# Splitting the first norm's statistics between two engines, and reordering two steps of the last image, in a four-layer convolution network

## The chip, the cores and the metric

The kernel runs on one core of a Trainium2 chip. The metric is the device time of one execution in microseconds (us); the time before is the median of three runs, 3094.22 us (3093.67 to 3095.54). All data is fp32. The core's engines each work through their own queue of instructions in order: TensorE (PE, with its weight loads shown as PEld), VectorE (DVE), ScalarE (ACT), GpSimd (POOL) and SyncE (SP, which here only issues DMA transfers).

## The reference, cut to what matters

Four images of 256 channels and 64x64 pixels pass through four residual layers. What the change touches are two group norms inside layer 0 (`gn1` and `gn2`, eight groups of 32 channels each), the `_gn` between layers 0 and 1 (32 groups of 8 channels), and the inverse norms of the pixels in layer 1 (`rmsnorm`).

```python
def group_norm(x, w, b):                      # layer 0, 8 groups
    mean = xg.mean(axis=(2, 3, 4)); var = xg.var(axis=(2, 3, 4))
    return (xg - mean) * rsqrt(var + 1e-5) * w + b

# layer 0
xs = relu(group_norm(conv3x3(x, smooth_w) + smooth_b, gn1_w, gn1_b))
f = theta(xs) @ phi(xs)                       # 4096 x 4096 per image
y = softmax(f, axis=-1) @ g(xs)
out0 = group_norm(conv1x1(y, w_w, w_b), gn2_w, gn2_b) * 0.1 + xs
# layer 1
xn = rmsnorm(x, g_norm)                       # x / |x| over the channels of a pixel
q, k, v = conv1x1(xn, w_qkv)
out1 = rmsnorm(w_out @ linear_attention(softmax_d(q), softmax_n(k), v) + b_out, g_out)
# layer 2: a depthwise and a 1x1 convolution with generated weights; layer 3: mixed experts
x = x + out0(_gn(x)); x = x + out1(_gn(x)); x = x + out2(_gn(x)); x = x + out3(_gn(x))
```

## The kernel before

**Tiles.** 256 channels are two halves of 128 partitions (`NH = 2`); an image is 4096 columns per half. A k4 tile holds 128x1024 fp32, from a ring of nine; PSUM banks hold 128x512, a ring of eight. The order of the instructions on every engine is the order in which the program writes them down (a manual schedule); nothing is reordered afterwards.

**Stages.** `convolve_first` makes the 3x3 convolution of image 0 alone, since nothing else is there to run; `project` makes theta, phi and g; then `attend(b)` runs the 4096x4096 attention of image b in 8 blocks of 512 columns. Beside `attend(b)` runs a chain with the later layers of image b-1 and the convolution of image b+1. Behind the last image's attention there is no other attention: `tail` of image 3 (`nonlocal_out`, `linear_attention`, `generated`, `mixed`) runs alone, with the 16 pieces of image 2's layer 3 (`held`, matmuls into `ps_ex`) handed in by `w.fill(n)` to give PE something to do, and added to the result on DVE by `w.settle()`.

**The end of `convolve_first`.** The image's rows lie as `image[:, oh, :, k, :]`, four sets k of 16 rows for each channel half oh. After the last products, DVE joins row set 4 into the image (`rows_joined(4, oh, ...)`, six operations of 128x1024 for each half), then runs 12 `bn_stats` (128x512 each, for k = 0, 1, 2), four additions of the last products from PSUM (`tt(y, y, ps, ...)`, for k = 3), and 4 more `bn_stats`. `normed_relu` then calls `group_finish`: `bn_aggr` per half (L339), the bias added to the mean (L124), a matmul with an averaging matrix for the mean over the group (`pm`, L344), the deviations (`ev`), a matmul for the variance (`pv`, L355), and a power of -0.5 on POOL (L217). The affine factors follow, then the ReLU on ACT (L676), and `project` (L879).

**The last image's second norm.** `group_finish(wy_stats[b], ...)` runs as above on the attention's output, with the last two products of the output with the residual (`multiply`, L905, DVE 128x512 each) put in between. The mean and variance of the sum (norm output + residual), which the next norm (`_gn` of layer 1) needs, are not measured but worked out from the two means, variances and their covariance: about 20 DVE operations of 128x2 each, between the first norm's factor `rstd` and the next norm's `pm`. In them both the mean and the variance are complete (L1050 to L1055, tile `mv_in`; the profile shows them under the helpers L124 and L127) before `pm` starts. Two `bn_aggr` of the residual (L1043, `rmv`) lie there too. The addition itself (`on_the_way`, 128x512 and 128x1024 pieces on DVE) is done step by step by `next(sums)`.

**The loop over q, k, v.** `linear_attention` takes the image in 8 chunks of 512 columns. For each: `normed(c)` (ACT: two 128x512 normalisations L1102, a square L1104; DVE: the sum `s2`), `norms` (PE: eight small matmul instructions into `ps_ss`, L1112; DVE: a maximum, L1114; POOL: power -0.5, L217), `qkv` (PE: four products into `ps_qkv`, L1126; ACT: Exp and copy with the inverse norms `rinv` as scale, L1130 and L1131; DVE: sums and scaling of q, L1136 and L1137), and `context` (PE L1145, L1148). From chunk 1 on `norms` is called one chunk ahead. For chunk 0 it is called inside `qkv`, so that its DVE maximum stands behind what the loop's first pass has put into DVE's queue:

```python
        for c in range(NC):
            if c + 1 < NC:
                ahead = normed(c + 1)
            if alone:
                next(sums, None)
            yield 0.5
            this = yield from qkv(*ready)
```

`alone` is true for the last image only.

Of the kernel before, what the change touches and what calls it, by code (L numbers as in the profile page):

```python
# [8 lines left out]
F32 = mybir.dt.float32  # L9
# [84 lines left out]
def conv_preact_fast(ctx: ExitStack, tc: tile.TileContext, guard, x, wc, wtpg, ww, wqkv, wout, w1cat, wd2,  # L94
# [25 lines left out]
    def bank(name):  # L120
        return pp.tile([P, 512], F32, tag="bank", name=name, bufs=8)

    def tt(o, a, b, op):
        nc.vector.tensor_tensor(o, a, b, op)  # L124

    def stt(o, a, s, b, op0, op1):
        nc.vector.scalar_tensor_tensor(o, a, s, b, op0, op1)  # L127
# [199 lines left out]
    def stats_tile():  # L327
        return sp.tile([P, NH, 8, 6], F32, name="st")

    def group_finish(st, avg, eps, shift=None, between=()):  # L330

        if callable(st):
            mv = st()
        else:
            mv = sp.tile([P, NH, 2], F32, name="mv")
            for h in range(NH):
                nc.vector.bn_aggr(mv[:, h, :], st[:, h, :, :].rearrange("p c s -> p (c s)"))  # L339
        if shift is not None:  # L340
            tt(mv[:, :, 0], mv[:, :, 0], shift, ALU.add)
        yield 1
        pm = bank("pm")
        nc.tensor.matmul(pm[:, 0:NH], avg, mv[:, :, 0], start=True, stop=True)  # L344
        gm = sp.tile([P, NH], F32, name="gm")
        nc.vector.tensor_copy(gm, pm[:, 0:NH])
        ev = sp.tile([P, NH], F32, name="ev")
        tt(ev, mv[:, :, 0], gm, ALU.subtract)
        tt(ev, ev, ev, ALU.mult)
        tt(ev, ev, mv[:, :, 1], ALU.add)  # L350
        for f in between[0:1]:
            f()
        yield 1
        pv = bank("pv")
        nc.tensor.matmul(pv[:, 0:NH], avg, ev, start=True, stop=True)  # L355
        rstd = sp.tile([P, NH], F32, name="rstd")
        nc.vector.tensor_scalar(rstd, pv[:, 0:NH], eps, None, ALU.add)  # L357
        rsqrt(rstd, rstd)
        for f in between[1:]:
            f()  # L360
        return mv, gm, rstd
# [451 lines left out]
    def convolve_first(w):  # L813

        def go(ops):
            for op, *args in ops:
                op(*args)

        def across_all(a, rows):
            return [(a, k, across_plain(k, rows), lambda oh, h, k=k: u[a](k, oh, h)) for k in ACROSS1]  # L820

        filter_down((0,))
        _, gm, rstd = yield from input_stats()
        yield from normalise(gm, rstd)
        st = stats_tile()
        products, joined, row_products, rows_joined, _, stats = joiner(st)
        keep((0,))
        go(down_plain(0, ra))
        filter_down((1, 2))
        go(down_plain(1, rb))  # L830
        filter_down((5,))
        filter_down((3, 4))
        u = {a: filter_across(a) for a in (2, 4, 3)}
        keep((1, 2, 5, 3, 4))
        copy_x(0)

        for t in (rb, rc):
            nc.gpsimd.memset(t[:, :, :, 0:1], 0.0)
            nc.gpsimd.memset(t[:, :, :, HW + 1:HW + 2], 0.0)
        row_products(0, ra)  # L840
        go(down_plain(2, ra, rb))
        row_products(1, rb)
        go(down_plain(3, rc))
        last = [(a, k, products(a, k, v, f)) for a, k, v, f in across_all(2, ra)]
        for row, rows in ((3, rc), (4, rb)):
            this = across_all(row, rows)
            if row == 3:
                go(down_plain(4, rb, rc))
            else:
                go(down_plain(5, ra))  # L850
            for i, (a, k, v, f) in enumerate(this):
                if i + 1 < TX1:
                    t = joined(*last[i + 1])
                this[i] = (a, k, products(a, k, v, f))
            if row == 3:
                for oh in range(NH):
                    rows_joined(2, oh, t[oh])
            last = this
        y3 = row_products(5, ra)
        for i in range(1, TX1):  # L860
            t = joined(*last[i])
        for oh in range(NH):
            rows_joined(4, oh, t[oh])
        for j in range(3):
            stats(j)
        for y, ps in y3:
            tt(y, y, ps, ALU.add)
        stats(3)
        yield from normed_relu(w, 0, st)


    def project():
# [21 lines left out]
    res_st = cp.tile([P, NH, NQ, 6], F32, name="res_st")  # L894
    joint = cp.tile([P, NH, NQ], F32, name="joint")
    pivot_in = cp.tile([P, NH], F32, name="pivot_in")
    last_block = []

    def attend(b):

# [73 lines left out]
        for i in range(NQ * NM):  # L974
            q, m = divmod(i, NM)
            if m == 0:
                py = bank("py")
                tot = k4("tot")
            if i + 1 < NQ * NM:
                logits(i + 1)  # L980
            for s in range(2):
                nc.tensor.matmul(py, g[:, bass.ts(2 * m + s, P)], probs[i][:, bass.ts(s, 512)],  # L982
                                 start=(m == 0 and s == 0), stop=(m == NM - 1 and s == 1))
            if m == 1:
                tt(tot, probs[i - 1], probs[i], ALU.add)
            elif m > 1:
                tt(tot, tot, probs[i], ALU.add)
            if b == B - 1 and m == 9:
                xc = k4("xc").rearrange("p (h n) -> p h n", h=NH)
                nc.sync.dma_start(out=xc, in_=xs_d[b].rearrange("h p n -> p h n")[:, :, bass.ts(q, 512)])  # L990
            if b == B - 1 and m in (12, 14):
                h = m // 2 - 6
                nc.vector.bn_stats(res_st[:, h, q, :], xc[:, h, :])
            for t in todo:
                next(t, None)
            if m == NM - 1:
                todo = [ended(q, py, tot, xc)]
                next(todo[0])
            yield i + 1 < NQ * NM
# [6 lines left out]
    def nonlocal_out(w, b, big, k4, xs_in):  # L1006
# [26 lines left out]

        if xs_in is not None:

            mv = sp.tile([P, NH, 2], F32, name="mv_in", bufs=1)
            rmv = sp.tile([P, NH, 2], F32, name="rmv", bufs=1)
            cov = sp.tile([P, NH], F32, name="cov", bufs=1)
            off = sp.tile([P, NH], F32, name="off_in", bufs=1)
            tt(mv[:, :, 0], wmv[:, :, 0], bias, ALU.subtract)  # L1040
            tt(off, mv[:, :, 0], pivot_in, ALU.add)
            for h in range(NH):
                nc.vector.bn_aggr(rmv[:, h, :], res_st[:, h, :, :].rearrange("p c s -> p (c s)"))  # L1043
            nc.vector.tensor_reduce(cov, joint, AX.X, ALU.add)
            tt(off, off, rmv[:, :, 0], ALU.mult)
            stt(cov, cov, 1.0 / N, off, ALU.mult, ALU.subtract)
        sc, sh = affine(gm, rstd, vec_s[:, V_G2W, :], vec_s[:, V_G2B, :], bias, 0.1)
        if xs_in is not None:
            w.fill(1)
            tt(mv[:, :, 0], mv[:, :, 0], sc, ALU.mult)  # L1050
            tt(mv[:, :, 0], mv[:, :, 0], rmv[:, :, 0], ALU.add)
            tt(mv[:, :, 1], wmv[:, :, 1], sc, ALU.mult)
            stt(mv[:, :, 1], cov, 2.0, mv[:, :, 1], ALU.mult, ALU.add)
            tt(mv[:, :, 1], mv[:, :, 1], sc, ALU.mult)
            tt(mv[:, :, 1], mv[:, :, 1], rmv[:, :, 1], ALU.add)  # L1055

            def on_the_way():

# [14 lines left out]
                        added(2 * c + h, sc)  # L1073
                    yield

            return (lambda: mv), sh, on_the_way()
        w.fill(2)
        for i, (c, h) in enumerate(PARTS):
            added(i, sc)
# [10 lines left out]
    def linear_attention(w, b, big, qT, k4, st, sh, sums):  # L1090

        alone = sums is not None
        _, gm, rstd = yield from group_finish(st, avg8, 1e-5, sh, (lambda: next(sums),) * 2 if alone else ())
        nb = norm_bias(gm, rstd, sh)
        pctx = bank("ps_ctx")
        NC = N // 512
# [18 lines left out]
            rsqrt(rinv, rinv)  # L1115
            return rinv

        def qkv(xg, s2, rinv):

            qk = k4("qk").rearrange("p (j o) -> p j o", j=4)  # L1120
            v1 = k4("v1")[:, 0:4 * (P + 1)].rearrange("p (j o) -> p j o", j=4)
            nc.gpsimd.memset(v1[:, :, P:P + 1], 1.0)
            for j in range(4):
                ps = bank("ps_qkv")
                for h in range(NH):
                    nc.tensor.matmul(ps[:, 0:3 * HID], xg[:, h, bass.ts(j, P)], wqkv_s[:, h, :],  # L1126
                                     start=(h == 0), stop=(h == NH - 1))
                if rinv is None:
                    rinv = norms(s2)
                nc.scalar.activation(qk[:, j, :], ps[:, 0:2 * HID], AF.Exp, scale=rinv[:, j:j + 1])  # L1130
                nc.scalar.activation(v1[:, j, 0:P], ps[:, 2 * HID:3 * HID], AF.Copy, scale=rinv[:, j:j + 1])  # L1131
                yield 0.125
# [19 lines left out]
            w.fill(1)  # L1152
        w.settle()
        ahead = normed(0)
        if alone:
            next(sums)
        yield 1
        ready = *ahead, None
        last = None
        for c in range(NC):  # L1160
            if c + 1 < NC:
# [448 lines left out]
    def tail(b, big, qT, k4=k4, diag=None, xs_in=None, held=None):  # L1610

        def layers(w):
            st, sh, sums = yield from nonlocal_out(w, b, big, k4, xs_in)
            st = yield from linear_attention(w, b, big, qT, k4, st, sh, sums)
            st, sh = yield from generated(w, b, big, k4, st, sh, diag)
            if b + 2 < B:
                load_x(b + 2)
            elif b + 2 == B:
# [642 lines left out]
```

## Time and profile before

| | us |
|---|---|
| median of three runs | 3094.22 (3093.67 to 3095.54) |
| the profiled execution, its time | 3093.8 |
| its span, first to last instruction | 3091.9 |
| PE busy | 3001.9 (97%) |
| DVE busy | 2130.8 (69%) |
| ACT busy | 1152.7 (37%) |
| POOL busy | 131.9 (4%) |

Times in the views below count from the span's start. In a row of the timeline the first number is the start, the second the length from the first start to the last end, then engine, line, operation, output<-inputs, shapes, count; the bracket gives how long the engine had been idle before it and whose end released it. The mean granted TensorE clock of the execution is 0.993. Outside the two stretches that the change touches (118 to 143 us, and 2816 to 2864 us) the profile shows DVE, ACT and PE working through the attention at a steady pace.

### The profile page before, as it was taken

The page shows a single profiled execution, that of the slowest core. Times are in us where ns is not written, and L with a number is a line of the kernel's source. Part 1 is how long each engine was busy: PE and PEld are TensorE (multiplying, and loading weights), DVE is VectorE, ACT ScalarE, POOL GpSimd, SP SyncE. Part 2 cuts the span into 40 slices and gives each one's busy share as a digit, 9 for nine tenths or more (in the row PEclk, how much of TensorE's full clock was granted, in tenths as well). Part 3 has the DMA queues.
Part 4 walks back from the last instruction along what each step waited for, and adds up shares of the span by engine and source line. Part 5 has one row for each costly group of instructions (what it writes and reads, how often), then busy time and mean ns, then how long its engine had stood idle before and what let it go on. Part 6 is the DMA issues. An engine that isn't in the chain of part 4 may idle for free.

```text
span 3091.9 us, 24448 instructions
## 1 busy us (share of the span) xinstructions
PE 3001.9 (97%) x8606; PEld 1484.7 (48%) x8606; DVE 2130.8 (69%) x2773; ACT 1152.7 (37%) x2139; POOL 131.9 (4%) x178
## 2 busy tenths in 40 slices
PE   6899999999999999999999999999999999998998
PEld 3354555445554444444565444444546544444643
DVE  8747777853547996777536797678463669875485
ACT  2134333353555332323364432222346443333621
POOL 0100000000010000000011000000001100000100
PEclk9999999999999999999999999999999999999999
DMA  5234011122100023113300101311420000022021
GB/s 219 78 100 142 31 45 38 34 51 72 58 11 28 14 75 125 35 41 65 116 1 11 35 19 70 126 41 38 95 82 14 18 28 28 14 89 82 8 68 66
DMA packets 61088, 178.44 MB, mean 58 GB/s; under 512 B 6560, under 2 KB 16544, under 8 KB 56736
## 3 DMA queue, kind: packets, MB, share of 16 engines
q1 hardware_dynamic: 56928, 160.04, 15.1%
q0 software_dynamic: 4032, 16.78, 2.9%
q8 instruction: 70, 1.15, 0.2%
q14 instruction: 58, 0.48, 0.1%
HBM read 115.45 MB, written 78.12 MB: 63 GB/s over the span
## 4 chain that ended last, share of the span: by engine, by line
PE 78%; DVE 15%; issue 5%; ACT 1%; POOL 0%; DMA 0%; POOLq 0%; ACTq 0%; DVEq 0%
PE pf L926 23%; PE py L982 22%; PE ps_qkv L1126 5%; PE ps_conv L504 4%; PE ps_tp L879 4%; DVE dw L127 4%; PE ps_ex L1574 3%; DVE tot L124 3%; PE ps_pw L1374 3%; PE ps_conv L576 2%; PE ps_g L884 2%; PE ps_wy L963 2%; PE ps_o L1201 1%; PE ps_dw L1419 1%; DVE big L127 1%
## 5 line engine op out<-in xcount | busy, mean ns | idle before, releaser
L927 ACT ACTIVATE pr<-pf 128x512 f32<-128x512 f32 x1024 | 604.0, 597 | 1195.4 <-PE pf L926 1148.8
L926 PE MATMUL pf<-tpg 128*128 128x512 f32 x2048 | 969.3, 596 | 2.9 <-ACT pr L927 2.9
L982 PE MATMUL py<-pr,tpg 128*128 128x512 f32 x2048 | 962.4, 592 | 2.5 <-ACT pr L927 2.3
L124 DVE TENSOR_TENSOR tot<-tot,pr 128x1024 f32<-128x1024 f32 x448 | 546.1, 1219 | 175.2 <-ACT pr L927 174.0
L982 PEld LDWEIGHTS py<-pr,tpg 128*128 128x128 f32 x2048 | 388.9, 190 | 494.7 <-issue 477.6
L926 PEld LDWEIGHTS pf<-tpg 128*128 128x128 f32 x2048 | 381.9, 190 | 438.2 <-issue 412.1
L127 DVE SCALAR_TENSOR_TENSOR dw<-xp,dk,dw 128x1008 f32<-128x1008 f32 x208 | 262.9, 1267 | 9.9 <-ACT dw L1366 7.0
L504 PE MATMUL ps_conv<-v,u 128*128 128x512 f32 x384 | 171.0, 593 | 3.6 <-DVE v L124 3.6
L1126 PE MATMUL ps_qkv<-wqkv_s,xg 128*128 128x384 f32 x384 | 129.9, 487 | 0.0
L124 DVE TENSOR_TENSOR tpg<-ps_g,bg_s 128x512 f32<-128x512 f32 x32 | 22.1, 691 | 145.6 <-PE ps_g L884 145.6
L879 PE MATMUL ps_tp<-big,wtpg_s 128*128 128x512 f32 x256 | 118.0, 605 | 3.0 <-ACT big L676 3.0
L504 PEld LDWEIGHTS ps_conv<-v,u 128*128 128x128 f32 x384 | 72.7, 190 | 96.4 <-issue 89.8
L217 POOL TENSOR_TENSOR rstd<-rstd,half 128x2 f32<-128x2 f32 x24 | 17.5, 730 | 2347.5 <-DVE rstd L357 2230.5
L955 DVE RECIPROCAL inv<-pss 128x512 f32<-128x512 f32 x31 | 103.9, 3351 | 5.5 <-PE pss L938 5.5
L1374 PE MATMUL ps_pw<-dw,pk 128*128 128x512 f32 x224 | 101.4, 592 | 0.0
L1126 PEld LDWEIGHTS ps_qkv<-wqkv_s,xg 128*128 128x128 f32 x384 | 72.2, 190 | 53.5 <-issue 9.8
L1136 DVE TENSOR_REDUCE qs<-qk 128x16 f32<-128x512 f32 x24 | 16.5, 686 | 117.4 <-ACT qk L1130 117.4
L880 ACT ACTIVATE tpg<-ps_tp,btp_s 128x512 f32<-128x512 f32 x64 | 43.8, 686 | 119.6 <-PE ps_tp L879 119.6
L879 PEld LDWEIGHTS ps_tp<-big,wtpg_s 128*128 128x128 f32 x256 | 47.9, 195 | 55.0 <-issue 50.6
L1203 ACT ACTIVATE junk<-ps_o 128x256 f32<-128x256 f32 x128 | 49.1, 384 | 64.0 <-PE ps_o L1201 59.4
L1130 ACT ACTIVATE qk<-ps_qkv,rinv 128x256 f32<-128x256 f32 x96 | 45.5, 474 | 72.6 <-PE ps_qkv L1126 60.2
L124 DVE TENSOR_TENSOR v<-ra 128x1024 f32<-128x1024 f32 x58 | 69.6, 1221 | 0.4
(343 smaller groups left out, 3125.3 us busy)
## 6 DMA issues: line engine op xcount, KB each, us to landing
xp<-in_x_dram SPq DMA_DIRECT2D x16, 1024.0 KB, 6.4
wy_d<-wt SPq DMA_DIRECT2D x32, 512.0 KB, 2.9
wy<-wy_d SPq DMA_DIRECT2D x32, 512.0 KB, 4.0
out_dram<-res SPq DMA_DIRECT2D x64, 256.0 KB, 2.0
xs_d<-big POOLq DMA_DIRECT2D x24, 512.0 KB, 11.4
u<-filters SPq DMA_DIRECT2D x48, 256.0 KB, 2.5
xs<-xs_d SPq DMA_DIRECT2D x24, 512.0 KB, 4.8
u<-rows_d SPq DMA_DIRECT2D x36, 256.0 KB, 3.0
```

The costliest lines, as they stand in the source:

```text
L124: nc.vector.tensor_tensor(o, a, b, op)
L127: nc.vector.scalar_tensor_tensor(o, a, s, b, op0, op1)
L504: nc.tensor.matmul(ps[oh], u(oh, h), v[:, bass.ts(h, 512)], start=(h == 0), stop=(h == NH - 1))
L576: nc.tensor.matmul(ps[:, bass.ts(oh, IY * IX)], u[i][:, h, bass.ts(oh, P)], v[:, i, bass.ts(h, IY * IX)], start=(h == 0), stop=(h == NH - 1))
L879: nc.tensor.matmul(ps, wtpg_s[:, h, k, :], big[:, h, cols], start=(h == 0), stop=(h == NH - 1))
L926: nc.tensor.matmul(pf, phi[:, bass.ts(2 * m + s, P)], theta[:, bass.ts(q, 512)], start=True, stop=True)
L927: nc.scalar.activation(pr[:, bass.ts(s, 512)], pf, AF.Exp)
L955: nc.vector.reciprocal(inv, pss)
L982: nc.tensor.matmul(py, g[:, bass.ts(2 * m + s, P)], probs[i][:, bass.ts(s, 512)], start=(m == 0 and s == 0), stop=(m == NM - 1 and s == 1))
L1126: nc.tensor.matmul(ps[:, 0:3 * HID], xg[:, h, bass.ts(j, P)], wqkv_s[:, h, :], start=(h == 0), stop=(h == NH - 1))
L1374: nc.tensor.matmul(ps, pk[:, h * NH * P + oh * P:h * NH * P + (oh + 1) * P], dw[h][:, bass.ts(s, 512)], start=(h == 0), stop=(h == NH - 1))
L1574: nc.tensor.matmul(ps, wm[h][:, bass.ts(oh, P)], big[:, h, bass.ts(c, 512)], start=(h == 0), stop=(h == NH - 1))
```

## The change

Three parts. First, `convolve_first`: DVE takes `bn_stats` of the row sets 0 and 3 only. For each half, right after its join, the two `bn_stats` of row set 0 are aggregated into a `pivot`, whose negated mean is the bias of two ACT passes (Identity and Square) over each of the row sets 1 and 2, summed by the accumulator into `sums`. `moments` combines the two sources; `group_finish` takes it in place of the statistics tile. Second, for the last image, the residual's `bn_aggr` and two constants (`residual_known`) are moved into the attention's last block; the mean of the sum is worked out first and given to `pm`, the variance is worked out by `late()` behind `pm`, and the shift `sh` in the `between` step of the second norm. Third, for the last image, the first chunk's first product and its `norms` are written ahead of the loop.

```diff
+    def aggregated(st):
+        mv = sp.tile([P, NH, 2], F32, name="mv")
+        for h in range(NH):
+            nc.vector.bn_aggr(mv[:, h, :], st[:, h, :, :].rearrange("p c s -> p (c s)"))
+        return mv
...
+        mv, late = st() if callable(st) else aggregated(st), None
+        if isinstance(mv, tuple):
+            mv, late = mv
...
         nc.tensor.matmul(pm[:, 0:NH], avg, mv[:, :, 0], start=True, stop=True)
+        if late is not None:
+            var = late()
+        else:
+            var = mv[:, :, 1]
...
-        tt(ev, ev, mv[:, :, 1], ALU.add)
+        tt(ev, ev, var, ALU.add)
...
+        def half(oh, k):
+            for s in range(2):
+                nc.vector.bn_stats(st[:, oh, k // 3 * 2 + s, :], image[:, oh, bass.ts(s, IY // 2), k, :])
+
         for oh in range(NH):
             rows_joined(4, oh, t[oh])
-        for j in range(3):
-            stats(j)
-        for y, ps in y3:
+            half(oh, 0)
+            nc.vector.bn_aggr(pivot[:, oh, :], st[:, oh, 0:2, :].rearrange("p c s -> p (c s)"))
+            nc.vector.tensor_scalar(minus[:, oh:oh + 1], pivot[:, oh, 0:1], -1.0, None, ALU.mult)
+            for k in (1, 2):
+                for i, f in enumerate((AF.Identity, AF.Square)):
+                    nc.scalar.activation(k4("about").rearrange("p (y x) -> p y x", x=HW), image[:, oh, :, k, :], f,
+                                         bias=minus[:, oh:oh + 1], accum_out=sums[:, i, oh, k - 1:k])
+        for i, (y, ps) in enumerate(y3):
             tt(y, y, ps, ALU.add)
-        stats(3)
-        yield from normed_relu(w, 0, st)
+            if i == NH:
+                half(0, 3)
+        half(1, 3)
+
+        def moments():
...
+            for h in range(NH):
+                nc.vector.bn_aggr(mv[:, h, :], st[:, h, 0:4, :].rearrange("p c s -> p (c s)"))
+            nc.vector.tensor_reduce(both, sums, AX.X, ALU.add)
+            nc.vector.tensor_scalar(both, both, 1.0 / N, None, ALU.mult)
+            mean, var = mv[:, :, 0], mv[:, :, 1]
+            tt(mean, mean, minus, ALU.add)
+            tt(sq, mean, mean, ALU.mult)
+            tt(var, var, sq, ALU.add)
+            stt(var, var, 0.5, both[:, 1, :], ALU.mult, ALU.add)
+            stt(mean, mean, 0.5, both[:, 0, :], ALU.mult, ALU.add)
+            tt(sq, mean, mean, ALU.mult)
+            tt(var, var, sq, ALU.subtract)
+            tt(mean, mean, minus, ALU.subtract)
+            return mv
...
+    def residual_known():
+        nc.vector.tensor_scalar(factors[:, 0, :], vec_s[:, V_G2W, :], 0.1, None, ALU.mult)
+        nc.vector.tensor_scalar(factors[:, 1, :], vec_s[:, V_G2B, :], 0.1, None, ALU.mult)
+        res_mv.append(sp.tile([P, NH, 2], F32, name="rmv", bufs=1))
+        for h in range(NH):
+            nc.vector.bn_aggr(res_mv[0][:, h, :], res_st[:, h, :, :].rearrange("p c s -> p (c s)"))
+        tt(res_shift, res_mv[0][:, :, 0], factors[:, 1, :], ALU.add)
...
                 nc.vector.bn_stats(res_st[:, h, q, :], xc[:, h, :])
+                if q == NQ - 1 and h == NH - 1:
+                    residual_known()
...
+            tt(off, wmv[:, :, 0], pivot_in, ALU.add)
+            tt(off, off, bias, ALU.subtract)
             nc.vector.tensor_reduce(cov, joint, AX.X, ALU.add)
             tt(off, off, rmv[:, :, 0], ALU.mult)
             stt(cov, cov, 1.0 / N, off, ALU.mult, ALU.subtract)
-        sc, sh = affine(gm, rstd, vec_s[:, V_G2W, :], vec_s[:, V_G2B, :], bias, 0.1)
+            tt(off, wmv[:, :, 0], gm, ALU.subtract)
+            tt(sc, rstd, factors[:, 0, :], ALU.mult)
+            tt(off, off, sc, ALU.mult)
+            tt(mean[:, :, 0], off, res_shift, ALU.add)
             w.fill(1)
-            tt(mv[:, :, 0], mv[:, :, 0], sc, ALU.mult)
...
+            def variance():
+                tt(var, wmv[:, :, 1], sc, ALU.mult)
+                stt(var, cov, 2.0, var, ALU.mult, ALU.add)
+                tt(var, var, sc, ALU.mult)
+                tt(var, var, rmv[:, :, 1], ALU.add)
+                return var
+
+            def shift():
+                tt(sh, bias, gm, ALU.subtract)
+                tt(sh, sh, sc, ALU.mult)
+                tt(sh, sh, factors[:, 1, :], ALU.add)
...
-            return (lambda: mv), sh, on_the_way()
+            return (lambda: (mean, variance)), (sh, shift), on_the_way()
...
+        def product(xg, j):
+            ps = bank("ps_qkv")
+            for h in range(NH):
+                nc.tensor.matmul(ps[:, 0:3 * HID], xg[:, h, bass.ts(j, P)], wqkv_s[:, h, :], start=(h == 0), stop=(h == NH - 1))
+            return ps
...
-                ps = bank("ps_qkv")
...
+                ps = first if j == 0 and first is not None else product(xg, j)
                 if rinv is None:
                     rinv = norms(s2)
...
         ahead = normed(0)
+        ready = *ahead, None
         if alone:
+            first = product(ahead[0], 0)
             next(sums)
+            ready = *ahead, norms(ahead[1]), first
         yield 1
-        ready = *ahead, None
```

For the last image `group_finish` of the second norm is called with `between = (lambda: next(sums), at_last)`, where `at_last` runs `next(sums)` and then `shift()`; before, both entries were `next(sums)`.

More of the change, by code (lines that the diff above doesn't have):

```diff
@@ L328, in stats_tile @@
         return sp.tile([P, NH, 8, 6], F32, name="st")
-    def group_finish(st, avg, eps, shift=None, between=()):
[L334 to L339, printed above, removed]
+    def aggregated(st):
[3 more added lines that the diff above has]
+        return mv
+    def group_finish(st, avg, eps, shift=None, between=()):
+        mv, late = st() if callable(st) else aggregated(st), None
+        if isinstance(mv, tuple):
+            mv, late = mv
         if shift is not None:
@@ L861, in convolve_first @@
             t = joined(*last[i])
+        sums = sp.tile([P, 2, NH, 2], F32, name="sums", bufs=1)
+        pivot = sp.tile([P, NH, 2], F32, name="pivot", bufs=1)
+        minus = sp.tile([P, NH], F32, name="minus", bufs=1)
+        def half(oh, k):
+            for s in range(2):
+                nc.vector.bn_stats(st[:, oh, k // 3 * 2 + s, :], image[:, oh, bass.ts(s, IY // 2), k, :])
         for oh in range(NH):
             rows_joined(4, oh, t[oh])
-        for j in range(3):
-            stats(j)
-        for y, ps in y3:
-            tt(y, y, ps, ALU.add)
-        stats(3)
-        yield from normed_relu(w, 0, st)
+            half(oh, 0)
[6 more added lines that the diff above has]
+        for i, (y, ps) in enumerate(y3):
+            tt(y, y, ps, ALU.add)
+            if i == NH:
+                half(0, 3)
+        half(1, 3)
+        def moments():
+            mv = sp.tile([P, NH, 2], F32, name="mv")
+            both = sp.tile([P, 2, NH], F32, name="both_m", bufs=1)
+            sq = sp.tile([P, NH], F32, name="sq_m", bufs=1)
+            for h in range(NH):
[12 more added lines that the diff above has]
+            return mv
+        yield from normed_relu(w, 0, moments)
     def project():
@@ L896, in conv_preact_fast @@
     pivot_in = cp.tile([P, NH], F32, name="pivot_in")
-    last_block = []
+    last_block, res_mv = [], []
+    factors = cp.tile([P, 2, NH], F32, name="factors")
+    res_shift = cp.tile([P, NH], F32, name="res_shift")
+    def residual_known():
[5 more added lines that the diff above has]
+        tt(res_shift, res_mv[0][:, :, 0], factors[:, 1, :], ALU.add)
     def attend(b):
@@ L1034, in nonlocal_out @@
         if xs_in is not None:
-            mv = sp.tile([P, NH, 2], F32, name="mv_in", bufs=1)
-            rmv = sp.tile([P, NH, 2], F32, name="rmv", bufs=1)
+            mean = sp.tile([P, NH, 1], F32, name="mean_in", bufs=1)
+            var = sp.tile([P, NH], F32, name="var_in", bufs=1)
             cov = sp.tile([P, NH], F32, name="cov", bufs=1)
             off = sp.tile([P, NH], F32, name="off_in", bufs=1)
[L1040 to L1043, printed above, removed]
+            sc = sp.tile([P, NH], F32, name="sc_in", bufs=1)
+            sh = sp.tile([P, NH], F32, name="sh_in", bufs=1)
+            rmv = res_mv[0]
+            tt(off, wmv[:, :, 0], pivot_in, ALU.add)
+            tt(off, off, bias, ALU.subtract)
             nc.vector.tensor_reduce(cov, joint, AX.X, ALU.add)
@@ L1046, in nonlocal_out @@
             stt(cov, cov, 1.0 / N, off, ALU.mult, ALU.subtract)
-        sc, sh = affine(gm, rstd, vec_s[:, V_G2W, :], vec_s[:, V_G2B, :], bias, 0.1)
-        if xs_in is not None:
+            tt(off, wmv[:, :, 0], gm, ALU.subtract)
+            tt(sc, rstd, factors[:, 0, :], ALU.mult)
+            tt(off, off, sc, ALU.mult)
+            tt(mean[:, :, 0], off, res_shift, ALU.add)
             w.fill(1)
-            tt(mv[:, :, 0], mv[:, :, 0], sc, ALU.mult)
[L1051 to L1055, printed above, removed]
+            def variance():
[8 more added lines that the diff above has]
+                tt(sh, sh, factors[:, 1, :], ALU.add)
             def on_the_way():
@@ L1074, in on_the_way @@
                     yield
-            return (lambda: mv), sh, on_the_way()
+            return (lambda: (mean, variance)), (sh, shift), on_the_way()
+        sc, sh = affine(gm, rstd, vec_s[:, V_G2W, :], vec_s[:, V_G2B, :], bias, 0.1)
         w.fill(2)
@@ L1092, in linear_attention, with at_last @@
         alone = sums is not None
-        _, gm, rstd = yield from group_finish(st, avg8, 1e-5, sh, (lambda: next(sums),) * 2 if alone else ())
+        if alone:
+            sh, shift = sh
+            def at_last():
+                next(sums)
+                shift()
+            _, gm, rstd = yield from group_finish(st, avg8, 1e-5, None, (lambda: next(sums), at_last))
+        else:
+            _, gm, rstd = yield from group_finish(st, avg8, 1e-5, sh)
         nb = norm_bias(gm, rstd, sh)
@@ L1116, in norms, with qkv @@
             return rinv
-        def qkv(xg, s2, rinv):
+        def product(xg, j):
[3 more added lines that the diff above has]
+            return ps
+        def qkv(xg, s2, rinv, first=None):
             qk = k4("qk").rearrange("p (j o) -> p j o", j=4)
@@ L1123, in qkv @@
             for j in range(4):
-                ps = bank("ps_qkv")
-                for h in range(NH):
-                    nc.tensor.matmul(ps[:, 0:3 * HID], xg[:, h, bass.ts(j, P)], wqkv_s[:, h, :],
-                                     start=(h == 0), stop=(h == NH - 1))
+                ps = first if j == 0 and first is not None else product(xg, j)
                 if rinv is None:
@@ L1614, in layers @@
             st = yield from linear_attention(w, b, big, qT, k4, st, sh, sums)
-            st, sh = yield from generated(w, b, big, k4, st, sh, diag)
+            st, sh = yield from generated(w, b, big, k4, st, sh if sums is None else sh[0], diag)
             if b + 2 < B:
```

## The prediction

> **What bounds the kernel now.** I read the page first, for the engine that carries the span.
>
> ```profile
> span 3091.9 us, 24448 instructions
> PE 3001.9 (97%) x8606; PEld 1484.7 (48%) x8606; DVE 2130.8 (69%) x2773; ACT 1152.7 (37%) x2139; POOL 131.9 (4%) x178
> PE 78%; DVE 15%; issue 5%; ACT 1%; POOL 0%; DMA 0%; POOLq 0%; ACTq 0%; DVEq 0%
> ```
>
> PE is busy for 97%, so time is won only where PE waits: some 90 us in all. The change touches two of these places. The timeline of the first (end of `convolve_first`):
>
> ```profile
> 125.17 7.21 DVE L493 BATCH_NORM_STATS2 st<-big 128x6 f32<-128x512 f32 x12
> 132.29 2.46 DVE L124 TENSOR_TENSOR big<-big,ps_row 128x512 f32<-128x512 f32 x4
> 134.67 2.46 DVE L493 BATCH_NORM_STATS2 st<-big 128x6 f32<-128x512 f32 x4
> 137.98 0.56 PE L344 MATMUL pm<-mv,avg 128*128 128x2 f32 x2 [7.05 <-DVE mv L124]
> 141.75 4.63 ACT L676 ACTIVATE big<-big,sh,sc 128x1024 f32<-128x1024 f32 x4 [41.27 <-DVE sh L124]
> ```
>
> DVE is without a gap from 110.80 to 137.83, PE ended its products at 130.93, ACT has been idle for 41 us: DVE alone sets `pm`, and all behind it. The second place is the last image, where nothing runs beside it; DVE, ACT, POOL and PE rows of the timeline:
>
> ```profile
> 2833.80 0.38 PE L344 MATMUL pm<-mv_in,avg 128*128 128x2 f32 x2 [2.10 <-DVE mv_in L124]
> 2837.27 1.52 ACT L1102 ACTIVATE ra<-tpg,nb,rstd 128x512 f32<-128x512 f32 x2 [11.58 <-DVE nb L124]
> 2844.55 2.48 DVE L127 SCALAR_TENSOR_TENSOR tpg<-wy,sc,xp 128x1024 f32<-128x1024 f32 x2
> 2846.94 0.15 DVE L1114 TENSOR_SCALAR rinv<-ps_ss 128x4 f32<-128x4 f32 x1
> 2847.17 1.01 POOL L217 TENSOR_TENSOR rinv<-rinv,half 128x4 f32<-128x4 f32 x1 [10.07 <-DVE rinv L1114]
> 2848.21 0.47 ACT L1130 ACTIVATE rt<-ps_qkv,rinv 128x256 f32<-128x256 f32 x1 [4.31 <-POOL rinv L217]
> 2854.17 1.02 PE L1112 MATMUL ps_ss<-ones,s 128*128 128x1 f32 x8 [2.43 <-DVE s L124]
> ```
>
> The matmuls for chunk 0's norms ended at about 2841.6, but their maximum (L1114) ran at 2846.94, behind `s` of chunk 1 and two additions. ACT stood 4.31 us for it, so chunk 2's square came late, and PE stood 2.43 us at 2851.74. The table of busy time by window shows what that gap cost besides (busy us of PE, PEld, DVE, ACT and POOL, then the granted clock):
>
> ```profile
> 2848.60:2852.00 3.40, 3.14 (x10) 1.52 (x8) 1.34 (x3) 3.40 (x10) 0.00 (x0) 1.00 0.35 128
> 2852.00:2855.40 3.40, 1.23 (x11) 1.26 (x12) 1.05 (x3) 3.19 (x9) 1.06 (x2) 1.00 0.12 17
> 2855.40:2858.80 3.40, 3.40 (x14) 2.79 (x13) 1.70 (x4) 3.37 (x7) 1.06 (x2) 0.50 0.40 142
> ```
>
> The clock is 0.50 for the 3.4 us after the thin stretch.
>
> **Part 1, first norm.** Removed from DVE: 8 `bn_stats`, each 0.593 (7.12 from 125.17 to 132.29, by 12): 4.75. Added in the joins: for each half an aggregate (0.33) and a negation (0.16), each waiting for the one before it. From the start of the second `bn_stats` that is 0.68 + 0.37, and 0.08 on to the next independent operation: 1.13 against a pitch of 0.59, 0.54 more per half, 1.1 in all. Added at the end (`moments`): ten 128x2 operations; a dependent one has a pitch of 0.195 (138.77, 138.97, 139.16), an independent one 0.08 (2832.01 after 2831.94): seven dependent, three not, 1.6. Net -4.75 + 1.1 + 1.6 = -2.1.
>
> The new wait: `moments`' reduction waits for ACT, and behind it on DVE is all of the norm. An ACT pass with accumulator is not shown at 1024 elements; near it is the row with accumulator and bias at 512:
>
> ```profile
> 3007.55 0.72 ACT L1392 ACTIVATE junk<-tpg,pivot 128x512 f32<-128x512 f32 x1
> 3008.18 0.19 ACT L1392 ACTIVATION_READ_ACCUMULATOR junk<-tpg,pivot 128x1 f32 x1
> 3008.39 0.72 ACT L1392 ACTIVATE junk<-tpg,pivot 128x512 f32<-128x512 f32 x1
> ```
>
> Pitch 0.85. The same engine's 128x1024 square (1.056) against its 128x512 ones (0.63) gives 0.43 for 512 elements more: 1.28 a pass, 5.1 for the second half's four. They start when the second pivot is known: 118.0 + 1.7 (first half's pivot) + 7.2 (join) + 1.8 = 128.7, and end at 133.8. DVE meanwhile does four additions and four `bn_stats` (8 x 0.595) and two aggregates (0.55) and comes to the reduction at 133.9. ACT just fits. Lower bound 1.28; upper bound the costliest 1024-element row, 2.31 (L638, strided output) + 0.19 = 2.5: ACT would end at 138.7 and the part lose 2.7. The pass reads rows of 64 and writes contiguously, as L1366 (1.14), so I take 1.28. The first half's passes hide under the second join; the eight ring tiles were last read by matmuls and joins that are over. PE's last products (130.93) are needed by the fourth addition at 131.6: covered by 0.7.
>
> [...] By these rows [...]2.56 on ACT against 1.19 on DVE for the same 1024 elements. [...] But ACT is idle here and DVE sets the end, so the row's sum holds: **2.1 us**.
>
> **Part 2, second norm of the last image.** Until the second `multiply` (2830.10) the order is unchanged. After it DVE now has nine small operations to the mean instead of nineteen and two aggregates. From 2830.77, with the pitches above: two for `off`, reduction, `off`, `cov`, `off` come to 2831.50; POOL's `rstd` ended at 2831.39, so `sc` follows there, product and mean, end 2832.06, `pm` at 2832.1: 1.7 earlier than 2833.80. The four variance operations (0.78) lie beside `pm` (0.42) and push its copy by 0.1; `pv` 1.6 earlier. At `rstd` the shift's three operations (0.6) lie under POOL's power (1.1), nearly: `nb` ends at about 2835.75, ACT starts at 2835.8, **1.5 earlier**. The moved `residual_known` (about 1.0) goes into DVE's gap of 1.60 ahead of `tot` in the last block; without that cover it would cost up to 1.0. The issue of 4 output transfers and the `wy` loads on SP moves along, order unchanged.
>
> **Part 3.** DVE's order becomes: four `res` additions (2.75), `s` of chunk 0, two additions of 512, maximum of chunk 0, `s` of chunk 1, two additions of 1024 (2.48). The maximum now waits at the head for `ps_ss`, and behind it are `s` of chunk 1 and those additions. PE, with its order unchanged, is 1.46 earlier: `ps_ss` 2839.2 to 2840.1, while DVE comes free at 2840.4. So it waits for nothing; POOL ends at 2841.65. ACT does chunk 1's normalisation and square from 2839.85 to 2842.4 and goes on with Exp: no idle, 5.8 earlier than 2848.21. Chunk 2's normalisation waits for the second addition (2845.55), its square ends at 2847.4, `s` at 2848.1. PE, 1.46 earlier throughout, ends chunk 1 at 2850.3: `s` is there, the gap is gone. Behind, `ps_ss` to the end of chunk 2's products takes 9.24 now (2854.17 to 2863.41) and 7.33 one chunk later (2863.41 to 2870.74), all in order: the half clock's cost is 1.9. Gain for parts 2 and 3 together 1.46 + 2.43 + 1.91 = **5.8 us**. From 2863 the loop is PE-bound and moves as a whole.
>
> [...] The rows show 0.50 after 3.4 us in which PE was busy for 1.23, so I count it[...].
>
> **Sum.** 2.1 + 5.8 = 7.9 against the profiled execution's own 3093.8 (span 3091.9 and 1.9 around it): 3085.9. The median shown is 0.4 higher: 3094.22 - 7.9 = 3086.3.
>
> **Rivals.**
> - *Gain only in part.* The clock falls anyway, or fell only in some executions (-1.9), or ACT's passes run 0.3 longer each (-1.2): 3088.0 to 3089.0. For it: ACT's margin of 0.1. Against: the rows' pitches repeat to 0.01. 21%.
> - *The first norm gains nothing*[...]: 3088.4. Within it 3 of the 21%.
> - *DVE's head of queue blocks*: `ps_ss` late by PE at half clock (`ps_ex` 3.4 instead of 1.7). It would have to be over 1.2 us late before anything moves; each us costs one: 3087.5. 4%.
> - *Slower*: the ACT passes set the end. Place: `moments`' reduction. The part loses from 1.86 a pass (133.9 + 2.1 = 136.0, less 128.7, by four), the whole change from 3.3 a pass; at 2.5 the sum is still -3.1. It needs a price that no row has, some 3.8: 3096. 3%.
> - *It does as said*: 3086.3. 72%.
>
> **The numbers.** Likeliest 3086.3. Low end: part 1 at 2.5 and the loop at 6.6 (9.1): 3085.1. High end, through the partial case: 3088.6. A measurement of this kernel tells about 0.2%, 6.2 us, from no change, so faster begins at 3088.0: the likeliest case, the blocked queue and a share of the partial one lie below: 0.77. Within 0.2%: 0.20; slower 0.03.
>
> **What would show it.** Right: `pm` of the first norm near 135.8; ACT passes of 1.28; `nb` 1.5 earlier against the block's last `tot`; no idle on ACT ahead of the first Exp (L1130), none on PE at chunk 2's `ps_ss`, clock 1.00 through the loop. Wrong: DVE idle at `both_m`; DVE's L1114 waiting for `ps_ss`; a new gap of PE later in the loop that takes the 2.4 us back, or a fall of the clock elsewhere.

## The result, and the profile after

| | before | after |
|---|---|---|
| median, us | 3094.22 (11 runs, 3093.22 to 3096.09) | 3084.24 (11 runs, 3083.21 to 3086.76) |
| profiled execution, its time / span | 3093.8 / 3091.9 | 3084.23 / 3082.4 |

The ratio is 0.9968 (95% interval 0.996 to 0.9976): 10.0 us faster. The forecast was 7.9, and the range ended at 3085.1, so the sign was right and the size too small. The page of the changed kernel:

```profile
span 3082.4 us, 24468 instructions
PE 3000.3 (97%) x8606; PEld 1483.7 (48%) x8606; DVE 2128.5 (69%) x2780; ACT 1162.0 (38%) x2155; POOL 132.1 (4%) x178
PE 77%; DVE 16%; issue 5%; ACT 1%; POOL 0%; DMA 0%; POOLq 0%; DVEq 0%; ACTq 0%
```

PE does the same 8606 instructions and is busy for 1.6 us less; ACT has 9 us more work and DVE 2 less. The timeline of the first norm, DVE, ACT and PE rows:

```profile
119.44 0.21 DVE L884 BATCH_NORM_AGGREGATE pivot<-st 128x2 f32<-128x12 f32 x1
132.15 1.13 ACT L888 ACTIVATE about<-big,minus 128x1024 f32<-128x1024 f32 x1
133.19 0.19 ACT L888 ACTIVATION_READ_ACCUMULATOR about<-big,minus 128x1 f32 x1
133.33 0.38 DVE L902 BATCH_NORM_AGGREGATE mv<-st 128x2 f32<-128x24 f32 x2
133.62 0.10 DVE L903 TENSOR_REDUCE both_m<-sums 128x4 f32<-128x8 f32 x1
135.46 0.56 PE L348 MATMUL pm<-mv,avg 128*128 128x2 f32 x2 [4.40 <-DVE mv L124]
```

ACT's last pass is over at 133.38 and DVE takes the sums at 133.62 without a wait; `pm` starts at 135.46 instead of 137.98. The timeline of the last image:

```profile
2833.37 1.52 ACT L1182 ACTIVATE ra<-tpg,nb,rstd 128x512 f32<-128x512 f32 x2 [10.39 <-DVE nb L124]
2837.95 0.15 DVE L1194 TENSOR_SCALAR rinv<-ps_ss 128x4 f32<-128x4 f32 x1
2839.92 0.46 ACT L1214 ACTIVATE rt<-ps_qkv,rinv 128x256 f32<-128x256 f32 x1
2840.65 2.48 DVE L127 SCALAR_TENSOR_TENSOR tpg<-wy,sc_in,xp 128x1024 f32<-128x1024 f32 x2
2847.68 0.95 PE L1192 MATMUL ps_ss<-ones,s 128*128 128x1 f32 x8
```

The maximum (L1194) now runs ahead of the two additions, the first Exp follows with no idle bracket, and chunk 2's `ps_ss` has none either: PE's gap of 2.43 is gone. What was not forecast is the row of `ps_h`, in the last image's fourth norm. The timeline of before, and then of after:

```profile
2953.59 7.01 PE L1308 MATMUL ps_h<-tpg,w1n 128*32 128x512 f32 x31
```
```profile
2945.65 5.32 PE L1394 MATMUL ps_h<-tpg,w1n 128*32 128x512 f32 x31
```

The change doesn't touch these 31 instructions, but they are 1.7 us shorter. The granted clock says why: 0.50 from 2954.40 to 2957.82 before, 1.00 after. The table of busy time by window (columns as in the prediction's table, then DMA share and GB/s), before and then after:

```profile
2954.40:2957.82 3.42, 3.42 (x16) 1.14 (x13) 3.42 (x6) 1.23 (x3) 0.00 (x0) 0.50 0.26 102
```
```profile
2945.65:2950.97 5.32, 5.32 (x45) 1.79 (x39) 5.11 (x9) 2.58 (x5) 0.00 (x0) 1.00 0.41 117
```

To add this up, I cut every profile at the starts of the same instructions: DVE's first join (110.80 before), the first norm's `pm`, the last `tot` (DVE's last addition in the last image's attention), the last image's first `xg` (the normalisation on ACT that the profile shows as `ra<-tpg,nb,rstd`), `ps_ss` of chunks 2 and 3, `ps_pool` behind `ps_h`, and the row of the last matmuls, `count`. Lengths in us, from the timelines (e1 to e4 and e7 are experiments below):

| stretch | before | after | e1 | e2 | e3 | e4 | e7 (after again) |
|---|---|---|---|---|---|---|---|
| join to `pm` | 27.18 | 24.52 | 24.52 | 27.18 | 27.17 | 27.17 | 24.52 |
| `pm` to `tot` | 2679.94 | 2679.75 | 2679.87 | 2679.96 | 2680.20 | 2678.54 | 2679.90 |
| `tot` to `xg` | 19.35 | 18.16 | 19.35 | 17.91 | 19.36 | 18.35 | 17.92 |
| `xg` to chunk 2's `ps_ss` | 16.90 | 14.31 | 16.91 | 16.91 | 14.31 | 14.31 | 14.31 |
| to chunk 3's `ps_ss` | 9.07 | 7.34 | 9.07 | 7.41 | 7.34 | 7.34 | 7.34 |
| to `ps_pool` | 99.11 | 97.70 | 99.14 | 99.15 | 97.45 | 97.43 | 99.00 |
| to `count` | 123.28 | 123.27 | 123.39 | 123.03 | 122.91 | 122.85 | 122.99 |

The first, third and fourth rows hold what the new order brings by itself: 2.66 + 1.19 + 2.59 = 6.4 us. The others hold 3.3 us in stretches whose instructions keep their order, but for the moved `residual_known` (0.19, 1.73, 1.41, 0.01). The start up to the first join, the same in all the kernels here, took 0.14 longer; it lay between 110.76 and 112.18 us in the fourteen profiles, so it adds a scatter of up to 1.4 us to any comparison of whole times.

### The profile page after: what moved, and what is told of

Same layout as the page of the kernel before. It is cut to its first block, busy times and chain, and to the rows that moved or that the text cites. A ratio compares the mean times of both kernels' runs of the same rounds, so it can differ in the third digit from the quotient of the medians.

```text
span 3082.4 us, 24468 instructions
## 1 busy us (share of the span) xinstructions
PE 3000.3 (97%) x8606; PEld 1483.7 (48%) x8606; DVE 2128.5 (69%) x2780; ACT 1162.0 (38%) x2155; POOL 132.1 (4%) x178
## 3 DMA queue, kind: packets, MB, share of 16 engines
q8 instruction: 70, 1.15, 0.2%
## 4 chain that ended last, share of the span: by engine, by line
PE 77%; DVE 16%; issue 5%; ACT 1%; POOL 0%; DMA 0%; POOLq 0%; DVEq 0%; ACTq 0%
PE pf L984 22%; PE py L1040 22%; PE ps_qkv L1201 5%; PE ps_conv L512 4%; PE ps_tp L926 4%; DVE dw L127 4%; PE ps_ex L1660 4%; DVE tot L124 3%; PE ps_pw L1460 3%; PE ps_conv L584 2%; PE ps_g L931 2%; PE ps_wy L1021 2%; PE ps_o L1287 1%; PE ps_dw L1505 1%; DVE big L127 1%
```

## The experiments

Theory A: the parts add up stretch by stretch to 6.4 us, and the rest is PE's half clock (in the profile before, stretches of 3.41, 6.83 or 13.65 us, the one at the end of the span apart), and a shift of the instructions changes what falls into such stretches. Theory B: the rest too belongs to the new order. Each kernel ran beside the kernel before on the same chip; the median of before beside it stands in brackets. Where no clock is given for a run, it is read from the lengths of instructions that the profiles of before and after show at both: eight `ps_ctx` took 1.06 at 1.00 and 1.93 at 0.50, 31 `ps_h` 5.32 at 1.00 and 7.01 with 3.42 us of 0.50 in them, `pm` or `pv` 0.38 at 1.00 and 0.56 to 0.59 at 0.50.

**e1, e2, e3, e4: the parts one by one.** e1 takes only `convolve_first` from the changed kernel. e2 takes only the `variance`/`shift`/`residual_known` edits, and leaves out these lines, which with `product` and `first` in `qkv` make up e3; e4 is e2 and e3 together:

```diff
+            first = product(ahead[0], 0)
             next(sums)
+            ready = *ahead, norms(ahead[1]), first
```

> Part 1 alone (first norm's statistics split), the last image as before. Theory A (the parts add up stretch by stretch, and what lies beyond the sum is where TensorE's half-clock windows fall in the last image): the first norm's pm stands 2.5 to 2.7 us earlier, the last image's stretch from tot to chunk 2's ps_ss is as long as before (36.3 us), time 2.0 to 3.5 us shorter, with ps_h at half or full clock as its windows fall. Theory B (part 1 gains only what was forecast, and the rest comes from the last image's new order): 2.1 us, at most 2.3.

3091.76 (3093.70), ratio 0.9993 (0.9984 to 1.0001). The whole, 1.9 us, fits B's number better; the stretch is 2.66 shorter, as A has it, and the last image is as before to 0.02 up to chunk 3's `ps_ss`. In its profile the first join started 0.71 later than before (111.51), which hides part of the 2.66 in the whole. The runs of e1 differ by 2.5 us, those of before by 3.3 and those of e4 by 5.7, so a median alone does not decide this; the stretch does.

> Part 2 alone (second norm's mean ahead of its variance, residual's aggregates moved). Both theories: the first xg of the last image 1.2 us nearer to the last tot, chunk 0's maximum still behind two additions of 1024, ACT idle some 4.3 us ahead of the first Exp, TensorE's gap at chunk 2's ps_ss still 2.4 us. Theory A: time 0.5 to 2.0 us shorter. Theory B: likewise 1.2.

3091.89 (3093.70), 1.8 us. `xg` came 1.44 nearer to `tot`, the gap of 2.44 at chunk 2's `ps_ss` stayed. And yet the clock behind it was full, in the timeline and the table by window (first the row of before, then those of e2; the table's first row has the gap):

```profile
2855.62 1.93 PE L1148 MATMUL ps_ctx<-v,rt 128*128 128x129 f32 x8
```
```profile
2852.78 1.02 PE L1153 MATMUL ps_ss<-ones,s 128*128 128x1 f32 x8 [2.44 <-DVE s L124]
2853.66 0.64 PE L1190 MATMUL ps_qt<-ident,rt 128*128 128x128 f32 x4
2854.13 1.06 PE L1193 MATMUL ps_ctx<-v,rt 128*128 128x129 f32 x8
```
```profile
2849.10:2852.50 3.40, 1.24 (x4) 0.38 (x2) 2.26 (x5) 3.19 (x7) 1.06 (x2) 1.00 0.00 0
2852.50:2855.90 3.40, 3.12 (x23) 2.86 (x24) 1.50 (x4) 3.40 (x11) 0.00 (x0) 1.00 0.51 149
```

Before, the same eight `ps_ctx` instructions took 1.93 instead of 1.06. So the gap alone does not bring the half clock: PE was busy for 1.23 of the 3.40 us from 2852.00 before, with 0.50 behind them, and for 1.24 of the 3.40 us from 2849.10 in e2, with 1.00 behind them. What made the difference was not shown.

> Part 3 alone (first chunk's norms ahead of the loop). Theory A: first Exp 4.4 us nearer to the first xg, no gap of TensorE at chunk 2's ps_ss, no half clock behind it; time 3.5 to 5.0 us shorter if ps_h is at half clock as before, up to 1.7 more if it is not. Theory B: the last image's new order is what brings the part of the gain beyond the sum, so 5.5 us or more whatever the clock rows show.

3089.47 (3093.70), 4.2 us: A. The first Exp is 4.39 nearer to `xg`, and there is no gap. B's 5.5 in every execution is out.

> Parts 2 and 3 without part 1. Theory A: 5.5 us from tot to chunk 3's ps_ss, and in the whole 5.0 to 7.3, the upper end only where ps_h runs at full clock. Theory B: 7.2 or more in every execution.

3087.13 (3093.70), 6.6 us, and `ps_h` at full clock in its profile (31 in 5.32): A's upper end; the median does not reach B's 7.2. e2 and e3 sum to 6.0.

**e5, e6: keep PE busy in its waits (a miss).** Added to before and after, called in the waits:

```diff
+    def warm(ps, n):
+        for _ in range(n):
+            nc.tensor.matmul(ps[:, P:512], ww_s[:, 0:P], wtpg_s[:, 0, :, :].rearrange("p k o -> p (k o)"), start=True, stop=True)
...
         nc.tensor.matmul(pm[:, 0:NH], avg, mv[:, :, 0], start=True, stop=True)
+        warm(pm, keep[1])
```

> The kernel before, with matmuls of constants (128x384, results unread) put into TensorE's waits at the first norm, in the last image's second, third and fourth norm, ahead of chunk 2's ps_ss, at the end of the loop over outputs and in layer 3's norm: the waits stay, the work is unchanged, only TensorE is kept busy in them. Theory A (about 3 of the 10 us are TensorE's half clock[...]): no half clock from 130 to 160 us nor in the last image, so project starts 2.8 us faster, chunk 2 1.7, ps_h 1.7, the first products of layer 3 2.2: 7 to 10 us shorter than before. Theory B (the clock is a by-product and costs nothing on the path; the whole difference is the new order): within 1.5 us of before.

> The changed kernel with the same matmuls of constants in the same waits (fewer where the wait is shorter). Theory A: what is left between this and the kernel before with them is the order alone: 2.7 for the first norm and 3.8 up to chunk 2's ps_ss, 6.5 us, instead of the 9.6 between the two kernels without them; so this one is 4 to 7 us shorter than the changed kernel. Theory B: the difference stays at 9 to 10.

3098.71 and 3094.89 (3094.68): 4.0 slower, and no change. In the first norm `pm` and `pv` took 0.38 and 0.35 instead of 0.56 each, and `project`'s first eight `ps_tp` 3.97 in e6 and 5.40 in e5 instead of 6.46 before, but the constants went into free columns of `pm` and `pv`, and the readers of those tiles waited for all writes into them. DVE rows of e6's timeline:

```profile
136.77 0.16 DVE L360 COPY gm<-pm 128x2 f32<-128x2 f32 x1 [1.23 <-PE pm L125]
140.75 0.16 DVE L372 TENSOR_SCALAR rstd<-pv 128x2 f32<-128x2 f32 x1 [3.23 <-PE pv L125]
```

Against waits of 0.74 each in the changed kernel, that is 3.0 us lost in this norm alone. Neither theory is tested by them.

**e8, e9, e10: the same, with the constants behind `pm` and `pv` in a bank of their own**, `warm(bank("ps_warm"), n)`, in before (e8), after (e9, fewer where the wait is shorter or gone), and after with the first norm's waits only (e10).

> The kernel before with the matmuls of constants as in e5, but those behind pm and pv in a bank of their own, so that no reader of pm or pv waits for them. Theory A: no half clock from 130 to 160 us nor in the last image up to ps_pool; pm of the first norm where it was, ps_tp to ps_g 3.8 us instead of 6.3, chunk 2's ps_ss to chunk 3's 7.3 instead of 9.1, ps_h at full clock; 5 to 9 us shorter than before. Theory B: within 1.5 us of before.

> The changed kernel with the same matmuls of constants, likewise in a bank of their own. Theory A: the difference to e8 is the order alone, 2.7 for the first norm and 3.6 to 4.0 from tot to chunk 2's ps_ss, 6.0 to 7.0 us in all; 3 to 6 us shorter than the changed kernel. Theory B: 9 to 10 between the two.

> The changed kernel with matmuls of constants in TensorE's waits of the first norm only. Theory A: project starts at full clock, ps_tp to ps_g 3.8 us instead of 6.0, the rest of the kernel as in the changed one: 2.0 to 3.0 us shorter than it. Theory B: no difference, since ACT's normalisation sets the pace of project's start.

| kernel | median, us (before: 3094.80) | ratio to before, 95% |
|---|---|---|
| e8, before kept busy | 3085.52 | 0.997 (0.9959 to 0.9982) |
| e9, after kept busy | 3080.13 | 0.9952 (0.9939 to 0.9966) |
| e10, after, first norm only | 3081.94 | 0.9959 (0.9946 to 0.9973) |

The old order with its waits filled gains 9.3 us, nearly as much as the whole change. In e8's timeline chunk 2's `ps_ss` comes 0.20 nearer to `tot` than before, and behind it `ps_ctx` (1.06) and `ps_h` (5.32) are at full clock:

```profile
2849.39 2.10 PE L125 MATMUL ps_ss<-wtpg_s,ww_s 128*128 128x384 f32 x6
2851.79 1.05 PE L1122 MATMUL ps_ss<-ones,s 128*128 128x1 f32 x8 [0.30 <-DVE s L128]
2853.17 1.06 PE L1158 MATMUL ps_ctx<-v,rt 128*128 128x129 f32 x8
2949.62 5.32 PE L1323 MATMUL ps_h<-tpg,w1n 128*32 128x512 f32 x31
```

With the half clock out of these rows, the difference between the two orders shrinks from 10.0 to 5.4 us: B's 9 to 10 is out. It is below A's 6.0 too. The stretches give 2.66 for the first norm again (join to `pm` 27.09 and 24.43) and 3.77 from `tot` to chunk 2's `ps_ss`; 0.6 is lost again between `pm` and `tot` (2676.60 in e8, 2677.17 in e9); what takes it was not shown. Another 0.6 goes in small pieces, at the start and behind `ps_pool`. e9's five runs spread over 1.0 us, e8's seven over 2.2, the changed kernel's eleven over 3.6. e10 is 2.3 us under the changed kernel's first median and 3.9 under its second (that of e7, below), at or above what A gave it; `ps_tp` to `ps_g`, the start of `project`, took 3.8 instead of 6.0. PE rows of after and then of e10:

```profile
140.55 6.16 PE L926 MATMUL ps_tp<-big,wtpg_s 128*128 128x512 f32 x8 [3.05 <-ACT big L684]
```
```profile
139.98 3.97 PE L936 MATMUL ps_tp<-big,wtpg_s 128*128 128x512 f32 x8 [0.36 <-ACT big L694]
```

B's zero is out. e9 is the fastest version, 4.1 us under the changed kernel's first median.

**e7: the changed kernel again.**

> The changed kernel once more, on the same chip as the two with the constants. Theory A: 8.4 to 9.7 us shorter than before; from the join to pm 2.66 less again, from tot to chunk 2's ps_ss 3.4 to 3.8 less again; the rest of the difference to the kernel before equals what the half-clock windows hold of TensorE's work in each. Theory B: 9.5 or more, with ps_h at full clock in every profile of it.

3085.84 (3094.68), ratio 0.9968 (0.9956 to 0.998): 8.8 us, A. Same 2.66 and the same 14.31, but `ps_h` took 6.79 this time, near the 7.01 that it had with half clock before, so its stretch is 99.00 instead of 97.70:

```profile
2946.22 6.79 PE L1394 MATMUL ps_h<-tpg,w1n 128*32 128x512 f32 x32
```

Two executions of one kernel thus differ by 1.3 in this term. They differ elsewhere too: the first join started 0.83 later, and `tot` to `xg` was 0.24 shorter, with `pm` and `pv` at full clock (0.38 each, 0.59 in after).

**e11, e12: one wait each, in the kernel before.** e11 has three constants ahead of chunk 2's `ps_ss` (`norms(ahead[1], 3 if alone and c == 1 else 0)`), e12 one behind `pm` and two behind `pv` in the fourth norm.

> The kernel before with three matmuls of constants (1.9 us) in the one wait of TensorE ahead of chunk 2's ps_ss, nothing else. Theory A: chunk 2's ps_ss stands where it was against tot, no half clock behind it, so chunk 3's ps_ss comes 7.3 us after it instead of 9.1; the rest unchanged, so 1.7 us shorter in the executions in which the clock fell there before, 0.5 to 1.7 in the mean. Theory B: the 9.1 us were the order's (ps_ctx waiting for DVE), so they stay, and the time with them.

> The kernel before with three matmuls of constants in TensorE's waits of the last image's fourth norm (one behind pm, two behind pv), nothing else. Theory A: ps_h starts where it did against chunk 3's ps_ss and runs at full clock, 5.3 us instead of 7.0 for 31 instructions; 1.7 us shorter in the executions in which it was at half clock, 0.5 to 1.7 in the mean. Theory B: no change.

e11: 3091.18 (3093.72), ratio 0.9991 (0.9982 to 0.9999). Chunk 2's to chunk 3's `ps_ss` 7.41 instead of 9.07, with `ps_ctx` at full clock (1.06): A.

```profile
2853.91 1.02 PE L1119 MATMUL ps_ss<-ones,s 128*128 128x1 f32 x8 [0.21 <-DVE s L128]
2855.26 1.06 PE L1155 MATMUL ps_ctx<-v,rt 128*128 128x129 f32 x8
```

The whole, 2.5, is more than that one wait can give; in its profile project's start is 1.3 us shorter too (`ps_tp` to `ps_g` 5.03 instead of 6.30). e12: 3092.78 (3093.72), 0.9 us, ratio 0.9997 (0.9988 to 1.0005). Its timeline is the cleanest pair to the kernel before, since `ps_b` (the small matmuls just ahead of `ps_h`) starts within 0.05 of it:

```profile
2951.81 1.54 PE L125 MATMUL ps_warm<-wtpg_s,ww_s 128*128 128x384 f32 x4
2953.63 5.32 PE L1318 MATMUL ps_h<-tpg,w1n 128*32 128x512 f32 x31
```

Up to `ps_pool` it is 1.65 ahead; 0.9 is given back in layer 3's norm, where `pv` took 0.59 instead of 0.39 and twelve `ps_ex` 8.46 instead of 7.73. So the gain at `ps_h` was not kept whole. In the whole, 0.9 alone would not stand out from the runs; the row of `ps_h` is what shows A.

## Why the prediction was right and wrong

- **What bounds the two places: right.** DVE alone set the first norm's `pm`; the maximum's place in DVE's queue set the first Exp.
- **Part 1, 2.1: mechanism right, size too small.** 2.66 in after, e1 and e7, and again between e8 and e9. The mis-sized terms: each pivot cost 1.03 from its second `bn_stats` to the next operation, not 1.13 (aggregates of 12 values took 0.21, not 0.33): 0.2; the two last aggregates took 0.29, not 0.55 (24 values instead of 48): 0.26; the remaining 0.1 lies in the smaller terms and the rounding. An ACT pass had a pitch (start to start) of 1.13, not 1.28: the L1392 row overstated it, the wait had 0.2 us to spare, and the rivals that rested on it fell. Two sums of these rivals are off: the part loses from (136.0 - 128.7) / 4 = 1.83 a pass, not 1.86, and a gain in part would end at 3087.5 to 3089.4, not 3088.0 to 3089.0; neither moves the likeliest case.
- **ScalarE against VectorE: the rows were right on the direction.** Two passes cost 2.26 on ACT (2.56 forecast) against 1.19 on DVE; moving the work to the idle engine still won 2.66.
- **Part 2, 1.5: 1.44 alone (e2), 1.19 in the whole change**, where `pm` and `pv` took 0.59 instead of 0.38 at half clock; in e7 both ran at full clock, and the gain was 1.43. The moved `residual_known` cost nothing (`pm` to `tot` 2679.96 in e2, 2679.94 before). **Part 3 up to chunk 2's `ps_ss`:** both together 3.89 forecast, 3.78 measured. DVE's maximum found `ps_ss` done, as worked out; ACT had no idle ahead of the first Exp.
- **The half clock behind the gap, 1.9: 1.73 in these two profiles, with half of the reason.** Before, PE was busy for 1.25 of the 3.41 us from 2852.01 to 2855.42, with most of the gap in them, and 0.50 followed. With the gap filled (e11) the clock stayed full (`ps_ctx` 1.06). The gap was not enough: e2 kept it (2.44) and ran at 1.00. So the 1.73 is partly luck; what it takes besides the gap was not shown. Among its rivals the forecast had a clock that falls only in some executions, and then counted this one fall alone.
- **The step that failed: "From 2863 the loop is PE-bound and moves as a whole."** The loop's instructions moved as a whole, the stretches of half clock did not (behind the loop 6.83 us from 2940.75 and 3.41 from 2954.40 before, 10.24 from 2930.82 after), and the forecast put what they do outside that loop at nothing. The stretch on `ps_h` fell out (1.7, of which 0.3 was lost just ahead of it), and project's start was 0.3 shorter. Sum of the profiles: 2.66 + 3.78 + 1.73 + 1.41 + 0.19 + 0.01 - 0.14 = 9.64 at `count`. The likeliest case had 7.9; of the 1.7 between them, 1.6 is the clock outside the loop and 0.6 is part 1, less 0.4 elsewhere. The low end, 9.1, was made of a bigger part 1 and a bigger loop and had no term for further stretches of half clock; it should have read every stretch at 0.50 in the profile as something that a shift can add or remove. The pace outside the two changed stretches was not as steady as the text ahead of the prediction has it: the profile before shows 0.50 also from 592.38, 2940.75, 2954.40, 3046.56 and 3087.52.
- **Luck.** In e7's runs the same kernel came to 3085.84, inside the forecast's range and with 8.8 us gained; the first eleven runs ended 0.9 us beyond it. Which stretches of half clock fall out in a given execution is not something that the forecast could have known.

What stays open: how often each stretch of half clock comes in either kernel. The medians gave 10.0 and 8.8 us for the same pair, so some 2.4 to 3.6 of the gain lies beyond the 6.4 of the stretches. In the profiles of before and after most of it is the clock (1.73 behind the gap, 1.41 up to `ps_pool`), but the start's scatter is in the medians too, and one profile of each can't say how the two share it.

## What to carry to other kernels

List the stretches of half clock in the profile before summing a change: one of 3.41 us cost up to 1.7 here (`ps_h`), and in the changed kernel, where `ps_h` comes 8 us earlier and some 90 us behind the last edit, it was gone in one profile (5.32) and not in the other (6.79). Where PE waits for a small chain on other engines, a few matmuls of constants into a bank of their own can be worth more than shortening the chain (9.3 us here for all the waits together, against 6.4). Where one engine alone holds up the others, work given to an idle one can pay even at twice the price (2.26 us on ACT against 1.19 on DVE, and 2.66 won), if it ends before the owner comes back for it.

## What the runs showed of the hardware

- In the profiles of before and after PE's granted clock was 1.00 or 0.50. Apart from the one at the end of the span, the stretches at 0.50 lasted 3.41, 6.83 or 13.65 us before and 3.41, 6.83 or 10.24 us after. In the 3.41 us ahead of each, PE was busy for 0.00 to 1.75 us before and for 0.00 to 2.00 after, at 1.00; a pause of 2.43 us (before, from 2851.74) lay ahead of one of them. The same was not always followed by 0.50: in e2 PE was busy for 1.24 of the 3.40 us from 2849.10, and the clock stayed 1.00.
- In after, ACT's accumulator read shows as 0.18 to 0.19 us (L888), but a 1024-element pass with it (1.13 to 1.15) had a pitch of only 1.13.
